# Side steps handed out by an account of the engines' time; context keys in column parts, value sums transposed

## The chip, the cores and the metric

The kernel runs on one core of a Trainium2 chip. A core has five engines with instruction streams of their own: TensorE (PE in the profile; its weight loads are shown apart as PEld), VectorE (DVE), ScalarE (ACT), GpSimd (POOL) and SyncE (SP), which here only issues transfers. Engines wait for each other by semaphores; each takes its instructions in order, so an instruction that waits holds everything behind it on that engine. The metric is the device time of one execution in microseconds, lower being better.

## The reference

One decoder layer over x of 16 batches x 256 positions x 512 columns, in float32:

```
x = x + mamba2(layernorm(x))                 # state space mixer, 32 heads of 64, state 64
x = x + attention(layernorm(x), context)     # 16 heads with sigmoid queries and keys
x = x + ffn(layernorm(x))                    # 512 -> 2048 -> 512, ternary weights, 8-bit activations

# mixer
xz = x @ W_in;  z, xBC, dt = split(xz)
xBC = silu(causal_conv4(xBC));  dt = softplus(dt + dt_bias);  A = -exp(A_log)
h_t = exp(A dt_t) h_(t-1) + dt_t x_t B_t;   y_t = h_t C_t + D x_t
y = norm_w * rms_normalised(y * silu(z));   out = y @ W_out

# attention
qh = sigmoid(q @ wq + bq);  kh = sigmoid(k @ wk + bk);  vh = k @ wv + bv
kv = einsum('bsh,bshd->bhd', kh, vh);  state = cumsum(kv, axis=1)       # over the heads
out = einsum('bsh,bhd->bshd', qh, state) @ wo + bo
```

## The kernel before

The 16 batches are worked in 8 pairs. The mixer's 2048 inner columns are cut into 16 units of 128, so its main loop has 128 slots (`for s in range(2, n_slots)`, L1927): slot s is unit s % 16 of pair s // 16. The last stage, the feed-forward layer (`ffn`, L1663), follows the 128 slots.

**A slot on TensorE**, in order: the projection of unit u0 to z (12 products of 512 columns, with the four transposes `trx` of the previous unit's x in the middle, L676 and L941); the projection to x (12 products); `scan_out` of the previous unit (`py`, L961 and L968); `out_product` of the one before (`po`, L1011, 12 products). **On VectorE**: `times_g` of the previous unit (L929, L933), `scan` of u0 (two scans, L912), three convolution taps on `xs` (L693), `plus_dx` (L976), `gated` (L981). ScalarE does the SiLUs, the convolution's first tap, the scaled copies `xdt` and `m`, the rounding `yh` and the squares; GpSimd does `yl` and the sum of squares.

**Side steps.** All other work of the layer lies between these: the norms of a later pair (`norm_pair`, L660), its time steps (`time_steps`, L698: with two long VectorE steps on tiles `sp_s`, L735 to L739, and `sp_q`, L742 to L745, and two exponentials on ScalarE that need another function table), its B and C states (`states`, L777: three taps on `bcT`, then `pg`, the products of B and C, L815), the end of a finished pair's batches (`batch_end`, L1049: norm, queries `q`, product `pa` with the attention's matrix z), the context keys and value sums (`context_pair`, L1201, and `context_group`, L1299), and the preparation of the feed-forward weights (`ffn_sums`, `ffn_quantised`). Each is a generator that yields before each step a wait, the points at which it may go on, an engine and a price in microseconds (helpers at L224 to L263).

**How they are placed.** The program is written out in full when it is built, and a slot has 8 points at which `advance(now)` (L1726) lets the generators issue steps. VectorE's steps may go at points 1, 2, 5 and 6, ScalarE's at 0, 5 and 6, GpSimd's at 2, 5 and 6, TensorE's at 3 (between the x projection and `scan_out`) and 7 (after the out product). `due` (L1714) holds a step back until its wait, a fixed distance of mostly 2 to 4 points after the step before, is over, and until its price fits what is left of its engine's budget (`room`: VectorE 2.3 us, ScalarE 2.5, TensorE 2.0, GpSimd 2.5); budgets are renewed at points 3 and 7. A step marked `leaves` (it empties a PSUM bank) is not held back by the budget. Transfers have a budget of their own.

**Banks.** Side products need a PSUM bank from `Banks` (L288): at point 7 one bank of their own, at most every half slot, in order of request; at point 3 they take, as "z", one of the two banks that the projections use in turn (`ps_p`). Then the next z projection uses the bank that the taps of the current x have just left. A pair's transposed input is held in two sets of tiles (`turned`), of which one is freed in slot 15 of each pair.

**Starting points.** `plan(s)` (L1763) starts the norms, time steps and states of pair k + 2 in slot 13 of pair k, the context pairs in slots 0 and 8 of the odd pairs, and a finished pair's batch ends in slot 2 of the next pair; `rank` orders the generators at each point.

**Context pair** (L1201 to L1296), for two batches: keys times weights in four column parts of the array (`pk`, L1225), moved to SBUF as `kp`; four products with `kp` as stationary and the 16 columns of `pick` streamed (L1246), which sum the four parts; a copy, tanh and scaling to `kh`; the key-weighted sums of the context in four column parts, one for each batch and half (`ptt`, L1264); a copy of 512 columns to `tt`; four products of `tt` with the selecting matrix `sel` (L1277), which transpose and add the halves, and the key sums (L1283); two copies into the group's tiles.

## Time and profile before

| what | value |
|---|---|
| median of three runs (lowest to highest) | 1882.19 us (1882.07 to 1885.43) |
| the profiled execution's own time | 1887.88 us |
| its span, first to last instruction | 1886.1 us |
| mean granted TensorE clock | 0.986 |
| PE, DVE, ACT, POOL busy | 95%, 87%, 66%, 36% of the span |
| pairs 1 to 6, length of each | 185.2, 190.2, 186.1, 185.2, 188.3, 183.4 us |
| the feed-forward stage | from about 1530 us to the end |

How to read it: busy is the time with an instruction of that engine in work, as the profiler has it. Matmuls overlap in a pipeline (a product of 512 columns is recorded with 0.38 us but starts every 0.217), so a busy PE may still lose time between starts. An idle time of an engine is put down to whatever released it last. Lengths of pairs are taken between the first `y<-xs,d_sb,py` (L976) of each.

### The profile page before, as it was taken

How to read it: one execution, taken by the hardware profiler on the slowest of the kernel's cores; microseconds unless marked ns; L12 is line 12 of the kernel's file. 1: busy time of each engine (PE TensorE's matmuls, PEld its weight loads, DVE VectorE, ACT ScalarE, POOL GpSimd, SP SyncE). 2: the span in 40 equal slices, each digit the busy share in tenths (PEclk: the TensorE clock that was granted, in tenths of full speed). 3: DMA queues.
4: the chain of work that ended last, by engine and by line, in shares of the span. 5: the costliest groups of instructions: out<-in, count | busy, mean ns of one | idle time of the engine just before them, and what ended most of it. 6: DMA issues, size and time to landing. Idle time of an engine off the chain costs nothing.

```text
span 1886.1 us, 30373 instructions
## 1 busy us (share of the span) xinstructions
PE 1786.5 (95%) x10464; PEld 1018.1 (54%) x10464; DVE 1638.2 (87%) x2711; ACT 1248.1 (66%) x2896; POOL 682.2 (36%) x691
## 2 busy tenths in 40 slices
PE   6789999998999998999999999998999989999998
PEld 4445555555556555555555555565656544444443
DVE  6989888777888889888988998989887888999997
ACT  5777666675666666666666666666666557777775
POOL 1233432344434354546454636463533222211000
PEclk8999999999999999999999999999999999999999
DMA  5764776788768777877597879787867734655454
GB/s 163 240 185 136 235 191 174 217 257 223 168 196 270 201 196 235 258 192 191 185 268 211 199 205 252 202 193 186 238 188 213 250 89 99 133 123 130 108 120 95
DMA packets 296933, 358.95 MB, mean 190 GB/s; under 512 B 163765, under 2 KB 197861, under 8 KB 296778
## 3 DMA queue, kind: packets, MB, share of 16 engines
q1 hardware_dynamic: 277962, 296.13, 60.0%
q0 software_dynamic: 18240, 60.84, 9.4%
q8 instruction: 83, 1.36, 0.3%
q14 instruction: 72, 0.59, 0.1%
q10 hardware_dynamic: 576, 0.04, 0.0%
HBM read 279.70 MB, written 39.58 MB: 169 GB/s over the span
## 4 chain that ended last, share of the span: by engine, by line
PE 57%; DVE 25%; DMA 7%; ACT 5%; issue 4%; POOL 2%; SPq 1%; ACTq 0%; POOLq 0%; DVEq 0%
PE pp L676 21%; PE po L1011 11%; PE po_f L1621 5%; PE pg L1579 4%; PE pu L1579 4%; DVE m L912 4%; DVE xs L693 4%; PE py L961 4%; DVE m L929 2%; PE trx L941 2%; DMA w<-w_d 2%; PE py L968 2%; DVE m L933 1%; DVE sp_q L742 1%; DVE y L976 1%
## 5 line engine op out<-in xcount | busy, mean ns | idle before, releaser
L676 PE MATMUL pp<-lnT_h_m,w 128*128 128x512 f16 (+1 forms) x2056 | 661.1, 383 | 23.3 <-DVE xs L693 20.8
L676 PEld LDWEIGHTS <-w 128*128 128x128 f16 x3084 | 296.5, 99 | 364.3 <-issue 35.8
L988 POOL TENSOR_TENSOR yl<-y,yh 128x512 fp32r<-128x512 f32 x128 | 178.9, 1398 | 717.5 <-ACT yh L987 659.3
L693 DVE SCALAR_TENSOR_TENSOR xs<-pp,convw_sb,xs 128x510 f32<-128x510 f32 (+2 forms) x384 | 286.1, 745 | 151.1 <-ACT xs L897 141.6
L676 PE MATMUL pp<-lnT_l_m,w 128*128 128x512 f16 (+1 forms) x1028 | 393.4, 383 | 0.0
L1011 PE MATMUL po<-wout,yh 128*128 128x512 f32 x1024 | 337.0, 410 | 4.6 <-DMA wout<-wout_d 4.6
L951 ACT ACTIVATE xdt<-trx,dt 128x64 f32<-128x64 f32 x1024 | 223.5, 328 | 167.4 <-PE trx L941 167.3
L912 DVE TENSOR_TENSOR_SCAN m<-dab,starts 128x512 f32<-128x512 f32 x254 | 302.2, 1230 | 0.5 <-DMA dab<-da_d 0.5
L1011 PEld LDWEIGHTS po<-wout,yh 128*128 128x128 f32 x1024 | 183.8, 189 | 61.3 <-issue 15.1
L1011 PE MATMUL po<-wout,yl 128*128 128x512 f32 x512 | 203.7, 398 | 3.0 <-POOL yl L988 3.0
L906 ACT ACTIVATE xs<-xs 128x512 f32<-128x512 f32 x128 | 80.9, 632 | 186.3 <-DVE xs L693 186.3
L961 PE MATMUL py<-m,xdt 128*64 128x256 f32 x1024 | 162.1, 395 | 11.1 <-DVE m L933 5.2
L1579 PEld LDWEIGHTS <-yT 128*128 128x128 bf16 x1024 | 100.0, 98 | 131.1 <-issue 14.7
L920 ACT ACTIVATE m<-edb,m 128x128 f32<-128x128 f32 x508 | 162.7, 395 | 12.1 <-DVE m L912 12.1
L999 POOL TENSOR_TENSOR ssq<-ssq,sq 128x512 f32<-128x512 f32 x120 | 158.6, 1321 | 27.9 <-ACT sq L998 27.0
L897 ACT ACTIVATE xs<-pp,convb_sb,convw_sb 128x512 f32<-128x512 f32 x128 | 100.3, 783 | 102.2 <-PE pp L676 102.1
L929 DVE TENSOR_TENSOR m<-m,g 128x1024 f32<-128x1024 f32 x128 | 161.9, 1265 | 0.1
L1579 PE MATMUL pg<-w_ffn,yT 128*128 128x512 bf16 x512 | 132.3, 381 | 4.7 <-ACT h L1583 4.7
L1579 PE MATMUL pu<-w_ffn,yT 128*128 128x512 bf16 x512 | 132.3, 381 | 4.6 <-DVE x L1037 4.6
L1621 PE MATMUL po_f<-w_ffn,hT 128*128 128x512 bf16 x512 | 125.4, 379 | 2.0 <-DMA hT<-hq 2.0
L1583 ACT ACTIVATE h<-pg,sg 128x512 f32<-128x512 f32 x128 | 86.6, 683 | 51.6 <-PE pg L1579 51.3
L1011 PEld LDWEIGHTS po<-wout,yl 128*128 128x128 f32 x512 | 96.7, 189 | 29.7 <-POOL yl L988 6.4
(278 smaller groups left out, 2791.9 us busy)
## 6 DMA issues: line engine op xcount, KB each, us to landing
dab<-da_d SPq DMA_DIRECT2D x127, 512.0 KB
wout<-wout_d SPq DMA_DIRECT2D x112, 512.0 KB
edb<-ed_d SPq DMA_DIRECT2D x127, 256.0 KB
w<-w_d SPq DMA_DIRECT2D x40, 512.0 KB
raw<-in_w_zx SPq DMA_DIRECT2D x16, 512.0 KB
wout_d<-wout SPq DMA_DIRECT2D x16, 512.0 KB
ctxT<-in_ctx_t POOLq DMA_DIRECT2D x16, 512.0 KB, 7.8
x<-in_x SPq DMA_DIRECT2D x16, 512.0 KB
```

The costliest lines, as they stand in the source:

```text
L676: nc.tensor.matmul(dst, w(wi, kc), yT[yi][:, :, kc, :], start=n == 0, stop=n == 3 * KD - 1)
L693: nc.vector.scalar_tensor_tensor(u[:, :, d:S], raw[:, :, 0 : S - d], w[:, j : j + 1], u[:, :, d:S], ALU.mult, ALU.add,)
L912: nc.vector.tensor_tensor_scan(u["m"][:, 4 * j : 4 * j + 4, :].rearrange("p k t -> p (k t)"), u["da"][j].rearrange("p h i t -> p (h i t)") ...
L920: nc.scalar.activation(u["m"][:, 8 + n, :], u["ed"][:, n // 2, n % 2, :], AF.Copy, scale=u["m"][:, 2 * n, P - 1 : P],)
L929: nc.vector.tensor_tensor(m, m, gi.unsqueeze(2).to_broadcast([P, 2, 2, NT * P]), ALU.mult)
L951: nc.scalar.activation(u["xdt"][:, j, i, h, :], u["tr"][:, j, i, h * HD : (h + 1) * HD], AF.Copy, scale=dt[:, i, j, 2 * c + h : 2 * c + h ...
L961: nc.tensor.matmul(py[h * HD : (h + 1) * HD, j, :].rearrange("p (i t) -> p i t", i=NT), xdt[:, j, 0, h, :], m[:, 2 * (2 * j + h) : 9 + 2 * ...
L988: nc.gpsimd.tensor_tensor(lo, u["y"], hi, ALU.subtract)
L999: nc.gpsimd.tensor_tensor(pair["ssq"], pair["ssq"], sq, ALU.add)
L1011: nc.tensor.matmul(pair["po"][n], u["yhl"][yi][:, j, i * P : (i + 1) * P], w[:, wi, :], start=c == 0 and p == 0, stop=c == NU - 1 and p == 2,)
L1579: nc.tensor.matmul(dst, yT[:, kc, :], w_ffn[w + kc][:, cols], start=kc == 0, stop=kc == KD - 1)
L1621: nc.tensor.matmul(u["po"], u["hT", k // (KF // 2)][:, k % (KF // 2), :], w_ffn[2 * KD + k // NF][:, (k % NF) * D : (k % NF + 1) * D], sta ...
```

## The change

**1. An account of the engines' time** (`Model`). While the program is written out, four clocks are kept for TensorE, ScalarE, VectorE and GpSimd. Each main operation of a slot adds its own duration, and starts no earlier than its inputs are reckoned to be ready; operations of VectorE that share SBUF access with GpSimd (`port`) and GpSimd's own don't overlap in it. From slot 18 to slot 127 (`modelled()`), a side step is handed out when `fits` says so: for VectorE when the next convolution taps still end by the end of the out products that cover them, for ScalarE and GpSimd when they stay within a bound behind TensorE, for TensorE when the inputs are reckoned ready and the taps stay in time (`Banks.take`). The slack grows with the slots that a step is overdue and near its task's `deadline`. The distances between steps become at most one point for steps of an engine, and the budgets are not asked any more, but for transfers; the points and the order of the banks stay. The prices in the steps themselves stay, too.

**2.** A pair's norms, time steps and states start in slot 12 instead of 13 (`AHEAD`).

**3.** `pg`, three products of 128 columns, becomes two: one of 256 and one of 128.

**4. Context pair**: `pick`, now 32 columns, becomes the stationary operand and `kp` is streamed, in four column parts; tanh reads PSUM; one transpose brings the keys back. The value sums are computed with columns instead of halves in the parts, accumulating over the halves, so that 256 columns are moved out instead of 512; two transposes take the place of the four products with `sel`, and four small copies that of two.

The diff, cut to its core (the other lines of the same kind: each main operation adds its duration with `model.op`, each `bank.take` names its product's duration, each `start` a deadline):

```diff
+        class Model:
+            def __init__(self):
+                self.t = dict.fromkeys(("pe", "act", "dve", "pool"), 0.0)
+                self.port, self.pool = [], []
+                self.proj, self.turn = [0.0, 0.0], 0
+                self.tp = 0.0
+            def op(self, engine, us, *after, port=False):
+                start_ = max([self.t[engine]] + [a + 0.1 for a in after])
+                if port:
+                    for a, b in self.pool[-6:]:
+                        if a <= start_ < b:
+                            start_ = b
+                            break
+                    self.port.append((start_, start_ + us))
+                elif engine == "pool":
+                    for a, b in self.port[-8:]:
+                        if a < start_ < b:
+                            start_ = b
+                            break
+                    self.pool.append((start_, start_ + us))
+                self.t[engine] = start_ + us
+                return start_ + us
+            def bank(self):
+                self.turn = 1 - self.turn
+                return 1 - self.turn
+            def convolved(self, dve, x_end):
+                return max(dve, max(x_end, self.t["act"]) + 0.9) + 2.3
+            def urgent(self, task):
+                return 0.5 * max(0, clock[0] / POINTS - task.deadline + 5)
+            def fits(self, task, moment, us):
+                t, e = self.t, task.engine
+                slack = 0.3 + 0.25 * max(0, clock[0] - task.due) / POINTS + self.urgent(task)
+                if e == "dve":
+                    if moment < 3:
+                        taps = self.convolved(t["dve"] + us, t["pe"] + X_US)
+                        end = t["pe"] + X_US + Y_US + OUT_US
+                    else:
+                        taps = self.convolved(
+                            t["dve"] + us + G_US + SCAN_US, t["pe"] + X_US + Z_US
+                        )
+                        end = t["pe"] + Z_US + X_US + Y_US + OUT_US
+                    return taps <= end + slack
+                if e == "act":
+                    return t["act"] + us <= t["pe"] + Z_US / 2 + 0.8 + slack
+                if e == "pool":
+                    return t["pool"] + us <= t["pe"] + (5.0 if moment > 3 else 9.0) + slack
+                return True
+        Z_US, X_US, Y_US, OUT_US, G_US, SCAN_US = 3.1, 2.6, 1.5, 2.85, 1.9, 2.45
+        model = Model()
+        current = [None]
+        def modelled():
+            return (NU + 2) * POINTS <= clock[0] < NP * NU * POINTS
...
-            def take(self, own=False, first=False):
+            def take(self, own=False, first=False, us=None, leaves_us=0.7):
                 me = [own]
+                task = current[0]
+                us = us or (task and task.pe_us) or 0.3
                 self.line.insert(0 if first else len(self.line), me)
+                asked = clock[0]
+                def fits():
+                    if not modelled():
+                        return True
+                    t, slack = model.t, 0.3 + 0.25 * (clock[0] - asked) / POINTS
+                    slack += model.urgent(task)
+                    if task.ready > t["pe"] + slack:
+                        return False
+                    if clock[0] % POINTS == 3:
+                        taps = model.convolved(t["dve"], t["pe"])
+                        return taps <= t["pe"] + us + Y_US + OUT_US + slack
+                    taps = model.convolved(
+                        t["dve"] + leaves_us + G_US + SCAN_US, t["pe"] + us + Z_US + X_US
+                    )
+                    return (
+                        self.free_at <= t["pe"] + slack
+                        and taps <= t["pe"] + us + Z_US + X_US + Y_US + OUT_US + slack
+                    )
                 while True:
                     moment = clock[0] % POINTS
                     if steady() and moment == 3:
                         others = [one for one in self.line if not one[0]]
-                        if self.free["z"] and others and others[0] is me:
+                        if self.free["z"] and others and others[0] is me and fits():
                             hold = "z"
                             break
                     elif self.free["own"] and self.line[0] is me and (
-                        not steady() or moment == 7 and clock[0] >= self.since
+                        not steady() or moment == 7 and clock[0] >= self.since and fits()
                     ):
                         hold = "own"
                         break
                     yield WAIT
...
-                for n, (s0, t0) in enumerate(((0, 0), (P, P), (0, P))):
+                for n, (s0, t0, t1) in enumerate(((0, 0, S), (P, P, S))):
                     nc.tensor.matmul(
-                        pg[:, n, :], bcT[0:NS, j, s0 : s0 + P], cT[:, j, t0 : t0 + P],
-                        start=True, stop=True,
+                        pg[:, 2 * n : 2 + n, :].rearrange("p n t -> p (n t)"),
+                        bcT[0:NS, j, s0 : s0 + P], cT[:, j, t0:t1], start=True, stop=True,
                     )
...
         def scan(u):
...
+                u["t_m"] = model.op("dve", 1.22, port=True)
...
+            hold = yield from bank.take(us=0.35)
+            pk = misc(hold, [P, P], f"pk2_{b}")
             for k in range(2):
                 for i in range(NT):
                     r = 64 * k + 32 * i
                     nc.tensor.matmul(
-                        pt[r : r + 32], kh[:, k, i, :], ct[k][:, i, :],
+                        pk[r : r + 32], pick, kp[:, k, i * P : (i + 1) * P],
                         start=True, stop=True, tile_position=(0, r),
                     )
-            yield leaves(dve(0.6))
-            tt = q1.tile([P, D], F32, tag="ttT", name=f"ttT_{b}")
+            yield leaves(act(0.3, 2))
+            khT = q1.tile([P, P], F32, tag="khT", name=f"khT_{b}")
+            nc.scalar.activation(khT, pk, AF.Tanh, scale=0.5)
+            bank.give(hold)
+            yield pe(0.2, 2)
+            hold = yield from bank.take(us=0.15)
+            pk = misc(hold, [P, 2, NT, 32], f"pk3_{b}")
+            nc.tensor.transpose(pk.rearrange("p k i h -> p (k i h)"), khT, ident)
+            yield leaves(dve(0.1))
+            nc.vector.tensor_scalar(
+                kh[:, :, :, 0:H], pk[:, :, :, 0:H], 0.5, 0.5, ALU.mult, ALU.add
+            )
+            bank.give(hold)
+            yield pe(0.5)
+            hold = yield from bank.take(us=1.0)
+            pt = misc(hold, [P, 2, P], f"ptt_{b}")
+            for i in range(NT):
+                for n in range(2):
+                    for k in range(2):
+                        r = 64 * n + 32 * k
+                        nc.tensor.matmul(
+                            pt[r : r + 32], kh[:, k, i, :],
+                            ct[k][:, i, :].rearrange("p (j n d) -> p n j d", j=2, n=2)[:, n],
+                            start=i == 0, stop=i == NT - 1, tile_position=(0, r),
+                        )
+            yield leaves(dve(0.4))
+            tt = q1.tile([P, 2, P], F32, tag="ttT", name=f"ttT_{b}")
             nc.vector.tensor_copy(tt, pt)
             bank.give(hold)
-            hold = yield from bank.take()
-            pt = misc(hold, [P, KD + 1, 4, 2, 4], f"ptk_{b}")
-            for kc in range(KD):
-                nc.tensor.matmul(
-                    pt[:, kc].rearrange("p q k h -> p (q k h)"), tt[:, kc * P : (kc + 1) * P],
-                    sel.rearrange("p q k h -> p (q k h)"), start=True, stop=True,
-                )
+            hold = yield from bank.take(us=0.6)
+            pt = misc(hold, [P, 2 * P + 2 * H], f"ptk_{b}")
+            for n in range(2):
+                nc.tensor.transpose(pt[:, n * P : (n + 1) * P], tt[:, n], ident)
+            sums = pt[0:1, 2 * P :].rearrange("p (k q h) -> p k q h", k=2, h=4)
             for k in range(2):
                 for i in range(NT):
                     nc.tensor.matmul(
-                        pt[0:1, KD, :, k, :], ones[:, 0:1],
+                        sums[:, k], ones[:, 0:1],
                         kh[:, k, i, 0:H].rearrange("p (q h) -> p q h", h=4),
                         start=i == 0, stop=i == NT - 1,
                     )
-            yield leaves(dve(0.2))
-            nc.vector.tensor_copy(
-                group["tt"][:, :, :, j : j + 2, :].rearrange("p c q k h -> p (c q) (k h)"),
-                pt[:, 0:KD].rearrange("p c q k h -> p (c q) (k h)"),
-            )
-            nc.vector.tensor_copy(group["ksum"][:, :, j : j + 2, :], pt[0:1, KD])
+            yield leaves(dve(0.3))
+            turned_ = pt[:, 0 : 2 * P].rearrange("p (c k q h) -> p c k q h", c=KD, k=2, h=4)
+            for k in range(2):
+                nc.vector.tensor_copy(
+                    group["tt"][:, :, :, j + k, :], turned_[:, :, k, 0:4]
+                )
+                nc.vector.tensor_copy(group["ksum"][:, :, j + k, :], sums[:, k])
             bank.give(hold)
             ctxs.give()
...
+            if task.engine and task.engine != "dma" and modelled():
+                if task.engine == "pe":
+                    if task.ready > model.t["pe"] + 0.3:
+                        return False
+                    task.pe_us = task.us
+                else:
+                    if not task.must and (
+                        task.ready > model.t[task.engine] + 0.2
+                        or not model.fits(task, now % POINTS, task.us)
+                    ):
+                        return False
+                    task.ready = model.op(task.engine, task.us, task.ready, port=task.port)
+                task.engine = None
+                return True
+            if modelled() and not task.engine and task.ready > model.t["pe"]:
+                return False
+            if task.engine == "pe":
+                task.pe_us = task.us
             if task.engine:
...
+                            task.port = task.engine == "dve" and not must
+                            if modelled() and task.engine and task.engine != "dma":
+                                wait = min(wait, 1)
+                            elif not task.engine and wait > 4:
+                                task.ready = 0.0
...
-            if (s == 1 or c == NU - 3) and k + ahead < NP:
+            if (s == 1 or c == NU - AHEAD) and k + ahead < NP:
                 pair = pairs[k + ahead] = {"k": k + ahead}
-                start(s, norm_pair(pair), rank=-4)
-                start(s, time_steps(pair), rank=-1 if k else -5)
-                start(s, states(pair), rank=-1)
+                first = (k + ahead) * NU
+                start(s, norm_pair(pair), rank=-4, deadline=first - 11)
+                start(s, time_steps(pair), rank=-1 if k else -5, deadline=first - 3)
+                start(s, states(pair), rank=-1, deadline=first)
...
-                    start(s, batch_end(batches[2 * ended["k"] + j]), rank=2)
+                    start(s, batch_end(batches[2 * ended["k"] + j]), rank=2, deadline=s + 12)
```

## The prediction

> **What bounds the kernel now.** First the clock: the core ran at a mean granted clock of 0.986, so there is no throttling to explain. Then the page's engine shares and slices, the stages in time, the waits of the stage that the change rewrites, and one bad slot beside a good one.
>
> ```profile
> PE 1786.5 (95%) x10464; PEld 1018.1 (54%) x10464; DVE 1638.2 (87%) x2711; ACT 1248.1 (66%) x2896; POOL 682.2 (36%) x691
> ```
>
> TensorE is the bound, with VectorE close behind. The change acts from slot 18 to slot 127 (about 280 to 1528 us). The stages there are the pairs 1 to 7, cut at the first `y<-xs,d_sb,py` of each; columns are stage, length, then busy us of PE, PEld, DVE, ACT and POOL:
>
> ```profile
> core 0: us, PE busy (x) PEld busy (x) DVE busy (x) ACT busy (x) POOL busy (x), PEclk, DMA share, GB/s
> 256.80:442.00 185.20, 178.04 (x1105) 105.61 (x1104) 144.00 (x204) 123.60 (x340) 67.51 (x77) 0.99 0.76 211
> 632.20:818.30 186.10, 177.97 (x1087) 106.31 (x1086) 164.75 (x231) 119.33 (x308) 91.01 (x90) 1.00 0.76 219
> 1191.80:1375.20 183.40, 176.80 (x1056) 105.37 (x1055) 165.40 (x235) 119.42 (x308) 89.60 (x80) 0.99 0.77 201
> 1375.20:1528.20 153.00, 151.05 (x888) 90.97 (x887) 132.01 (x189) 93.91 (x262) 44.88 (x37) 1.00 0.71 207
> ```
>
> A middle pair takes 183 to 190 us. Pair 7, with few side steps (15 slots up to 1528.2), runs at about 10.1 us a slot, or 161 for 16. The 25 us between them are side products on PE and waits. PE is uncovered for 6 to 8 us in each of the pairs 1 to 6, for 1.9 in pair 7. Who makes it wait between 280 and 1528 us (total, times, longest):
>
> ```profile
> PE pp L676 <- DVE xs L693: 20.2, 12, 3.4
> PE py L961 <- DVE m L933: 4.6, 5, 1.1
> PE po L1011 <- DMA wout<-wout_d: 4.6, 2, 4.3
> PE trx L941 <- ACT xs L906: 3.3, 4, 1.3
> PE pk L1246 <- DVE kp L1231: 2.4, 1, 2.4
> PE bc L676 <- ACT zs L891: 1.6, 1, 1.6
> ```
>
> So half of it is a projection that waits for VectorE's convolution taps. One such place in pair 6 (VectorE in order of time; then a quiet slot of pair 7):
>
> ```profile
> 1264.72 2.31 DVE L693 SCALAR_TENSOR_TENSOR bcT<-bc,convw_bc,bcT 128x510 f32<-128x510 f32 x3 [1.67 <-ACT bcT L791]
> ...
> 1268.68 3.37 DVE L912 TENSOR_TENSOR_SCAN m<-dab,starts 128x512 f32<-128x512 f32 x2
> 1271.97 1.25 DVE L735 TENSOR_SCALAR sp_s<-sp_v 128x128 f32<-128x128 f32 x1
> ...
> 1275.03 2.30 DVE L693 SCALAR_TENSOR_TENSOR xs<-pp,convw_sb,xs 128x510 f32<-128x510 f32 x3
> ...
> 1478.12 2.31 DVE L693 SCALAR_TENSOR_TENSOR xs<-pp,convw_sb,xs 128x510 f32<-128x510 f32 x3 [1.88 <-ACT xs L897]
> 1480.35 0.74 DVE L976 SCALAR_TENSOR_TENSOR y<-xs,d_sb,py 128x512 f32<-128x512 f32 x1
> ```
>
> Here 2.3 us of taps on `bcT` (must) and 3.1 us of `sp_s` (priced at 1.2) fell into one slot, and PE stood 3.44 us. PE then also runs slowly: the same 24 projections and 4 transposes took 5.41 us at clock 1.00 before this wait and 7.09 us at 0.76 after it:
>
> ```profile
> 1263.01:1268.42 5.41, 5.41 (x28) 2.73 (x28) 3.67 (x6) 5.35 (x14) 0.00 (x0) 1.00 1.17 169
> 1277.39:1284.48 7.09, 7.09 (x27) 3.46 (x28) 6.99 (x10) 5.47 (x14) 0.90 (x1) 0.76 0.43 157
> ```
>
> In the quiet slot VectorE idles 1.9 us even with a small side step. The taps end at 1480.4, the SiLU on them at 1481.15, the out products at about 1481.6, and the transposes that need the SiLU start at 1483.06: 1.9 us of slack.
>
> **The change part by part**, against the profiled execution (1887.88 us, span 1886.1; the three timed runs have a median of 1882.19, 5.7 lower; the same difference is taken off both).
>
> *The account: what it takes away.* The four waits it can see (20.2 + 4.6 + 3.3 + 2.4) are 30.5 us in 22 places. A wait is counted from the recorded end of the last matmul, 0.38 us after its start, where the next could start after 0.217: 0.17 hidden in each, 3.7 in all. The half speed after the long waits: 1.7 in the place shown, and by the starts of the projections about 0.8 after each of four more (two in pair 2, one each in 4 and 5): 5. Together 39. The two waits for `wout` stay, since transfers are not in the account.
>
> *What comes back.* The account uses the prices that stand in the steps. `time_steps` prices its two long VectorE steps at 1.2 and 1.7 us; the place above took 3.15 (1271.97 to 1275.12) and the second one 4.7 (1283.30 to 1288.03). The excess is 1.95 and 3.0 us. A step is accepted as long as the taps end by the end of the out products, so 1.2 to 1.5 of the 1.9 us slack may be used before it and 0.4 to 0.7 are left. Given at that limit the two cost PE 1.3 + 2.4 = 3.7 us a pair, given in an empty slot nothing; bounds 0 and 22 over six pairs, taken in the middle: +11.
>
> *Distances shortened.* Every wait of 2 to 4 points after an engine step becomes 1, so a side product on PE is issued as soon as its input is reckoned ready. Before, with 3 points between, side products waited for 2.4 + 1.6 + 0.7 (`pda` for ACT) + 0.5 (`q` for VectorE) = 5.2 us in the whole stretch. Behind a late one stand all of PE's products of the slot, then the taps and `plus_dx`. Bounds 0 and four times 5.2 = 21; I take +8, nearer the measured row because the points 3 and 7 lie 4 to 5 us apart and hide most errors.
>
> *Filling.* In pairs 3 to 6 VectorE is busy 165 us. If a pair shrinks from 185 to 177, its share is 93%, against 86% in pair 7 (132.01 of 153.00), where hardly a wait is left. Not every hole fits a step: bounds 0 and 10, taken +4.
>
> Together the account gives -39 + 11 + 8 + 4 = -16 us.
>
> *Context keys and value sums* (8 executions). Removed on PE: `pk2`'s 8 passes (729.83 to 730.75, 0.92 us) and `ptk`'s 8 passes with `sel` (771.32 to 772.23, 0.91). Added: four products of 128 columns in column parts. The nearest row is `ptt`, 512 columns in the same four parts in 1.00 us (760.34 to 761.34); a quarter is 0.25, at worst the 0.92 of what it replaces; I take 0.35. Also three f32 transposes at 0.11 (four `trx` in 0.43). `ptt` itself streams the same columns, 1.0. Net -1.83 + 0.35 + 0.33 = -1.15, times 8 = -9; bounds -10 and -5. VectorE: 0.21 + 0.32 + 0.67 + 0.28 + 0.17 go; 0.32, a 256-wide copy at 0.40 (the row `g<-pg,upper`), two of 64 at 0.21 and two `ksum` at 0.17 come: -0.2, nothing. ACT's tanh goes from 64 to 128 columns, 0.24 to 0.31: nothing, ACT is idle a third of the time. The extra bank turn and the ACT step between two PE steps are in the +8.
>
> The row for a column-part block's edges: from the last `ptt` product to the next main product it takes 0.2 us more than that one's spacing. [...]
>
> *`pg` in two products*: 6 passes took 742.74 to 743.60, 0.86; now 4 passes over the same columns: between 0.57 and 0.86, taken 0.70; 16 times, -2.
>
> *The rest.* AHEAD 4 starts the loads and norms of a pair a slot earlier. The transposed tiles are still freed only in slot 15, so nothing on the path moves. The step's 2.2 us on VectorE (priced 1.7), its POOL subtraction (2.15) and its SP load and transposes change place alone; SP waits there mostly for `dab` and `edb` buffers (272 and 269 us), which are two slots ahead. Cost 0; if that cover went, a late `lnT` would hold `time_steps` back and the taps would collide as now. POOL's own DMA issues (0.55 to 0.74 each) are not in the account; `yl` stands behind them, but 4 to 5 us before its product.
>
> The clock was 0.76 after the 3.44 us wait, but 1.00 (5.41 us again) after one of 2.67 us in pair 3. [...]
>
> Sum: -16 - 9 - 2 = -27. Profiled 1887.9 - 27 = 1861; median 1882.2 - 27 = 1855.
>
> **The rivals.**
>
> *Slower: the margin is spent everywhere.* Today a quiet slot has 1.9 us before the transposes. The account allows the taps to fall to the end of the out products in every slot that has side work (94 of them, 18 to 111). What it does not price (VectorE waiting for POOL: scans of 3.37 instead of 2.33, `sp` steps of 1.25 instead of 0.3) then reaches PE directly. A loss of w us in each takes the place of the +11: -39 - 9 - 2 + 8 + 4 + 94 w, which is nothing at w = 0.40 and decides from there on. At 0.5 us it is +9 (1891), at 0.6 +18 (1900), at 0.8 +37 (1919); I give it 1886 to 1919, around 1895. For it: VectorE at 89% in pairs 3 to 6. Against: 78% and 83% in pairs 1 and 2, and side work of VectorE averages under 2 us a slot where 2.5 are free.
>
> *A smaller gain: loads overtaken.* Transfers are not in the account. `ctx` lands a median of 7.7 us after its issue (at most 10.4), `wo` 7.3 (9.9). With one-point distances their products can follow a slot (10.1 us) later, POOL's issue itself may be late, and a wait for them holds all of PE. About 20 such products (6 `ctx`, 3 `wo`, some 12 `z`) at 0.5 to 1 us: +10 to +20, so 1865 to 1875. Against: the bank's line alone keeps steps two to four points apart.
>
> *A larger gain.* All waits but `wout` vanish: -39 - 5 - 9 - 2 = -55: 1827.
>
> *It does not do what it says.* Points and bank order stay as they are, so the steps may fall where they fell; then only the products count, and half of them hide in VectorE's slots: -5 to 0: 1877 to 1882.
>
> **How the numbers follow.** Forecast (1838 to 1868) 0.46; larger gain (1822 to 1838) 0.10; loads overtaken or little change of place (1868 to 1878) 0.14; within 0.2% (3.8 us, about what a measurement can tell) 0.07; slower 0.23, somewhat over a third of it (0.09) above 1893. The range 1832 to 1893 leaves out half the larger gain and that third, 0.14. The likeliest case's own range is 1838 to 1868. Faster 0.70, same 0.07, slower 0.23.
>
> **What would show it.** Right: pairs 3 to 6 at 179 to 183 us; the wait of the projections for `xs` under 8 us in the stretch; no stage with a clock of 0.76; in slots 4 to 8 of a pair `sp_s` no longer in the slot of the `bcT` taps; `pk` and `ptk` blocks of 0.3 and 0.6 us. Wrong: many waits of 0.5 to 1 us at `trx` for ACT `xs` (margin spent), waits at `ptt`, `zp` or `pa` for a DMA (loads overtaken), side steps left over beyond 1550 us, where VectorE is at 90% and above.

## The result: 1926 us, slower by 2.3%

The changed kernel takes 1926.49 us (median of six runs, 1924.13 to 1936.94), the kernel before, run beside it, 1884.15 (1882.07 to 1889.87): a ratio of 1.0229, 95% interval 1.0202 to 1.0256. The forecast was 1855, its range 1832 to 1893. The profiled execution took 1927.57 us against 1887.88, 39.7 more. Below, each run is given by its ratio to the kernel before, run beside it; "+17 us" means that ratio less one, times 1886.

The page's engine shares, then the stages (pairs 1, 3, 4, 6 and 7, cut as before; same columns) and the sum over pairs 1 to 7, all of the changed kernel:

```profile
PE 1789.4 (93%) x10456; PEld 1011.3 (53%) x10456; DVE 1660.9 (86%) x2717; ACT 1248.8 (65%) x2896; POOL 704.2 (37%) x690
```

```profile
256.30:453.00 196.70, 179.35 (x1098) 104.68 (x1097) 148.09 (x211) 124.35 (x342) 70.61 (x82) 0.96 0.72 210
...
651.50:845.60 194.10, 181.30 (x1147) 106.56 (x1146) 180.21 (x240) 125.84 (x316) 119.29 (x114) 0.98 0.80 234
845.60:1039.50 193.90, 179.81 (x1070) 106.54 (x1068) 178.73 (x252) 128.05 (x319) 115.49 (x104) 0.97 0.79 202
...
1228.10:1411.60 183.50, 175.84 (x1051) 104.45 (x1050) 161.09 (x224) 110.60 (x295) 55.06 (x45) 1.00 0.66 180
1411.60:1567.30 155.70, 150.71 (x885) 89.89 (x885) 132.08 (x187) 94.01 (x262) 47.76 (x37) 1.00 0.73 198
sum 1311.00, PE 1230.80 PEld 728.59 DVE 1120.39 ACT 833.21 POOL 579.97; mean PE 175.83 PEld 104.08 DVE 160.06 ACT 119.03 POOL 82.85
```

The seven pairs take 1311.0 us instead of 1271.4 (256.8 to 1528.2): the whole 39.6 us lie here. PE is busy for 1230.8 us, before for 1229.0, so the time is PE standing idle: 80 us instead of 42. Pairs 1 to 4 lose 8 to 12 us each; pair 6 is as before, pair 7 longer by 2.7. Who makes PE wait, between 275 and 1567 us of the changed kernel (total, times, longest):

```profile
PE pp L785 <- DMA w<-w_d: 13.7, 2, 11.0
PE trx L1060 <- ACT xs L1020: 12.1, 9, 2.8
PE pq L1151 <- POOL ssq L1125: 7.8, 2, 4.3
PE py L1083 <- DVE m L1050: 6.6, 5, 2.4
PE ptk L1409 <- ACT zs L1002: 4.6, 2, 2.8
PE pd L819 <- ACT zs L1002: 4.1, 1, 4.1
PE q L1206 <- DMA lnT_l_q<-lnl_q: 4.0, 1, 4.0
PE pp L785 <- DVE xs L802: 4.0, 6, 1.3
PE q L1206 <- ACT zs L1002: 3.2, 1, 3.2
PE kv L1456 <- ACT zs L1002: 3.0, 1, 3.0
```

With the smaller rows of the same view, grouped and set beside the view of before (us):

| what PE waits for | before | after |
|---|---|---|
| taps (`xs` of VectorE) | 20.2 | 4.0 |
| the rest of the scan chain (`trx`, `m`, `kp`) | 10.3 | 18.7 |
| a transfer (`w`, `wout`, `lnT`) | 6.1 | 20.5 |
| ScalarE's SiLU on z, by a side product (`zs`) | 2.3 | 18.2 |
| GpSimd's sum of squares (`pq`) | 0 | 7.8 |
| others | 1.9 | 8.4 |
| sum | 40.8 | 77.6 |

The account did what it was made for: the projections wait 4.0 us for taps, not 20.2. But all other waits together grew by 53 us. Two of them in the chain of waits. Late in pair 1 (start, length, what):

```profile
395.19 11.57 DMA z_d<-zh
...
406.82 13.63 DMA w<-w_d
...
420.49 2.74 PE pp L785 x6
```

SP's own queue shows why the load of `w` was issued so late, at 406.82:

```profile
394.50 3.43 SPq L1531 DMA_DIRECT2D z_d<-zh  x4
397.97 6.75 SPq L1531 DMA_DIRECT2D z_d<-zl  x4
...
406.82 0.83 SPq L521 DMA_DIRECT2D w<-w_d  x1
```

Eight stores of the attention's matrix z, issued in one point, take SP 10.2 us, and the load of `w` for the next projection stands behind them. By the chain, what let it go in the end was the landing of one of these stores, 11.57 us after its issue: SP's transfers wait here on eight semaphores in turn, mostly each for the transfer eight before it (the store issued at 395.19 and this load have the same one). In the kernel before, the load went 10 us ahead of the same stores:

```profile
395.76 0.42 SPq L412 DMA_DIRECT2D w<-w_d  x1
...
405.81 2.52 SPq L1400 DMA_DIRECT2D z_d<-zh  x4
408.43 4.52 SPq L1400 DMA_DIRECT2D z_d<-zl  x4
```

And in pair 4 of the changed kernel, the chain and then ScalarE's own row (in brackets its idle time and what ended it):

```profile
913.65 12.81 DMA wchunk<-in_w_up_t
...
928.10 1.53 ACT xdt L1072 x7
929.63 0.59 ACT zs L1002
...
930.26 0.77 PE q L1206 x24
```

```profile
926.48 1.52 ACT L1605 ACTIVATE wchunk<-wchunk,magic,wscale 128x512 f32<-128x512 f32 x2 [2.24 <-DMA wchunk<-in_w_up_t]
```

A chunk of the feed-forward weights lands 12.8 us after its issue. ScalarE has been given the step on it too early and waits 2.2 us, as it had waited 2.1 us for another chunk just before; behind these steps stand the main loop's `xdt` and the SiLU on z, and behind the SiLU stands PE, for 3.2 us, since its side product needs the bank that the SiLU empties. ScalarE's waits for these loads (same stretch) are 36 us in all, against 12 before; the three largest rows:

```profile
ACT wchunk L1570 <- DMA wchunk<-in_w_down_t: 12.1, 4, 5.8
ACT wchunk L1605 <- DMA wchunk<-in_w_gate_t: 10.6, 3, 4.9
ACT wchunk L1570 <- DMA wchunk<-in_w_up_t: 5.8, 4, 4.5
```

These steps are asked for six points after their load is issued (`landed(6)`), before as now. What is new is who lets them go: not a budget of ScalarE that other steps may have used up, but an account that gives them out as soon as ScalarE has time, by its reckoning; after a wait for a landing it sets `task.ready = 0.0`, that is, it takes the chunk to be there.

### The profile page after: what moved, and what is told of

Read it like the earlier page. It is cut to its first block, busy times and chain, and to the rows that moved or that the text cites. A ratio compares the mean times of both kernels' runs of the same rounds, so it can differ in the third digit from the quotient of the medians.

```text
span 1925.7 us, 30372 instructions
## 1 busy us (share of the span) xinstructions
PE 1789.4 (93%) x10456; PEld 1011.3 (53%) x10456; DVE 1660.9 (86%) x2717; ACT 1248.8 (65%) x2896; POOL 704.2 (37%) x690
## 4 chain that ended last, share of the span: by engine, by line
PE 50%; DVE 25%; DMA 7%; ACT 7%; issue 6%; POOL 4%; SPq 1%; ACTq 0%; POOLq 0%; DVEq 0%
PE pp L785 17%; PE po L1138 9%; PE po_f L1752 5%; PE pu L1710 5%; PE pg L1710 5%; DVE m L1027 5%; DVE xs L802 4%; PE py L1083 3%; DVE m L1046 2%; ACT xdt L1072 2%; PE trx L1060 2%; DVE y L1105 2%; PE py L1090 1%; DVE m L1050 1%; DMA w<-w_d 1%
## 5 line engine op out<-in xcount | busy, mean ns | idle before, releaser
L1113 POOL TENSOR_TENSOR yl<-y,yh 128x512 fp32r<-128x512 f32 x128 | 184.7, 1443 | 743.9 <-ACT yh L1112 653.7
L1027 DVE TENSOR_TENSOR_SCAN m<-dab,starts 128x512 f32<-128x512 f32 x254 | 324.3, 1317 | 0.0
L1036 ACT ACTIVATE m<-edb,m 128x128 f32<-128x128 f32 x508 | 164.3, 400 | 21.8 <-DVE m L1027 21.7
```

The source lines that it names most:

```text
L1027: nc.vector.tensor_tensor_scan(u["m"][:, 4 * j : 4 * j + 4, :].rearrange("p k t -> p (k t)"), u["da"][j].rearrange("p h i t -> p (h i t)") ...
L1036: nc.scalar.activation(u["m"][:, 8 + n, :], u["ed"][:, n // 2, n % 2, :], AF.Copy, scale=u["m"][:, 2 * n, P - 1 : P],)
L1113: nc.gpsimd.tensor_tensor(lo, u["y"], hi, ALU.subtract)
```

## The experiments

Four questions: which part costs (A), whether the unseen transfers do (B), what a mere change of the order of the side steps costs (C), and what is left when the account's blind spots are mended (D, E). "Moved" is how many of the 2650 to 2820 side instructions of pairs 1 to 7 lie in another slot than in the kernel before, counted from the two traces; where exactly a slot is cut shifts these counts by up to a tenth.

### A. The parts, each alone

`e1_products`: the changed kernel without the account and with the old starting slot.

```diff
 def modelled():
-    return (NU + 2) * POINTS <= clock[0] < NP * NU * POINTS
+    return False
-AHEAD = 4
+AHEAD = 3
```

> The column-part keys, transposed value sums and pg in two products, with the account never in force (budgets and distances as before, norms from slot 13). If the loss lies in the account, as the changed kernel's waits say, this is 4 to 11 us faster than before: 1873 to 1880, with the pk2 and ptk blocks on PE at 0.3 and 0.6 us. [...]

Measured 1923.42 us, 1.0178 (1.0147 to 1.0208): +34 us, where a gain of 4 to 11 had been expected if the loss lay in the account; 1715 steps moved.

`e7_account_only`: the changed kernel with the context pair, `sel` and `pg` of before.

```diff
-    pk = misc(hold, [P, P], f"pk2_{b}")
+    pk = misc(hold, [P, 2, NT, H], f"pk2_{b}")
...
-    pt = misc(hold, [P, 2, P], f"ptt_{b}")
+    pt = misc(hold, [P, D], f"ptt_{b}")
```

> The changed kernel's account and earlier start, with the context pair and pg of before. The products alone measured 36 us slower than before. Theory D (the longer chain of the context pair, one bank turn and one ScalarE step more, is what costs, and the account adds little): this is at 1880 to 1895. Theory A (steps handed out on weight chunks that have not landed): it is at 1905 to 1925, with ScalarE's waits on wchunk above 25 us. My forecast for the account alone was 16 us faster than before, 1870.

Measured 1924.2 us, 1.0205 (1.018 to 1.0231): +39; 1720 moved.

`e8_keys_only`: the kernel before, with the keys in column parts (one transpose and so one bank turn more).

```diff
-    pk = misc(hold, [P, 2, NT, H], f"pk2_{b}")
+    pk = misc(hold, [P, P], f"pk2_{b}")
...
+    nc.scalar.activation(khT, pk, AF.Tanh, scale=0.5)
+    bank.give(hold)
+    yield pe(0.2, 2)
+    hold = yield from bank.take()
+    nc.tensor.transpose(pk.rearrange("p k i h -> p (k i h)"), khT, ident)
```

> Before, with only the context keys in column parts (pk2, tanh from PSUM, the transpose pk3 with its own bank turn). Theory D: this part carries the loss of the products alone, +20 to +40 us, with a wait of PE for khT of some 10 us and the rest in side products that come a turn later. Theory E (any shift in the order of the side steps costs, since the chain of waits depends on where they meet): between +5 and +40, with waits in other places than in the products alone.

Measured 1929.05 us, 1.0225 (1.0183 to 1.0266): +42; 1765 moved. Its PE waits, first rows:

```profile
PE pp L676 <- DVE xs L693: 25.3, 10, 3.9
PE py L961 <- DVE m L933: 10.0, 5, 6.2
PE pk L1259 <- ACT khT L1254: 8.6, 2, 5.3
PE pd L710 <- DMA lnT_h_m<-lnh_m: 6.6, 1, 6.6
```

`e9_sums_only`: the kernel before, with the value sums turned.

```diff
-    pt = misc(hold, [P, D], f"ptt_{b}")
+    pt = misc(hold, [P, 2, P], f"ptt_{b}")
...
+    for n in range(2):
+        nc.tensor.transpose(pt[:, n * P : (n + 1) * P], tt[:, n], ident)
```

> Before, with only the value sums turned (columns in the parts, two transposes for the four products with sel, no bank turn more). Theory D: the products' saving alone, 0 to -6 us against before. Theory E: the different prices of two steps (0.4 for 0.6, 0.3 for 0.2) move some steps, and the time by +10 or more.

Measured 1888.35 us, 1.0003 (0.9986 to 1.002): +1; 77 moved.

The account and the keys each cost about as much as the whole change, so the parts don't add. The new product's own wait (`pk` for `khT`) is 8.6 us of the +42; the rest is spread over waits at other places. What the three dear runs share is that some 1700 side steps lie elsewhere. e8 alone doesn't separate this from a cost of the keys' longer chain of steps (one bank turn more).

The account alone (e7) does not lose at the places shown above: PE waits there 2.4 us for `zs` and 6.8 for transfers, hardly more than before, and 29.8 for the taps and the scan chain (before 30.5). The waits that grew in e7 are at many other places, 24.4 us instead of 1.9; the largest is 8.0 for GpSimd's `yl`. So the account loses about as much time in other ways when the order is another; what e7 loses by is not resolved here, though the mends of D bring it, too, down to +11 (e21).

### B. The transfers that the account doesn't see

`e2_landed14`: the changed kernel; the steps on weight chunks wait 14 points for their load (in both places).

```diff
     t = weight_chunk(k)
-    yield landed(6)
+    yield landed(14)
```

> The changed kernel, but the steps that load a chunk of feed-forward weights wait 14 points for it instead of 6. Theory A (ScalarE is handed steps on chunks that have not landed: 36 us of its waits on wchunk against 12 before, with xdt and the SiLU of z behind them): these waits fall below 8 us, PE's waits for zs and for trx fall by half, 1926 becomes 1890 to 1905. Theory B (side steps are packed too densely in pairs 3 and 4, so that VectorE and GpSimd slow each other: VectorE 179 to 180 us busy there against 165): it gains too, since chunks are spread over more slots, but with VectorE busy falling to 165 to 170. Theory C (the account hands out products at point 3 without asking whether the z bank is free): under 5 us gained, 1921 or more.

Measured 1907.1 us, 1.0093 (1.0062 to 1.0123): +18, just outside the 1890 to 1905 of theory A. ScalarE's waits for chunks are gone, and PE's waits for `zs` are 0.6 us instead of 18.2. Its waits for transfers stay, at 23.7.

`e3_no_landing`: the same order of steps, but the chunks are loaded to a place nobody reads.

```diff
-    nc.gpsimd.dma_start(t, src)
+    nc.gpsimd.dma_start(sink_d[k % 4], src)
...
-    t, t, AF.Abs, accum_out=...
+    t, starts.rearrange("p k t -> p (k t)"), AF.Abs, accum_out=...
-    nc.scalar.activation(t, t, AF.Identity, ...)
+    nc.scalar.activation(t, starts.rearrange("p k t -> p (k t)"), AF.Identity, ...)
```

> The changed kernel with the same order of steps, but the chunks of feed-forward weights are loaded into a scratch area in memory and ScalarE's steps on them read a constant tile, so that nothing waits for these loads; the feed-forward weights are therefore computed from constants. Theory A: ScalarE's waits on wchunk vanish and 15 to 30 us go with them, 1896 to 1911. Theory B: the density is the same, so VectorE stays at 178 to 180 us busy in pairs 3 and 4 and the time at 1915 to 1927.

Measured 1909.11 us, 1.0115 (1.0085 to 1.0146): +22. Here the order is that of the changed kernel (26 of 2570 steps lie in another slot), so the 21 us less by the ratios, 17 by the medians, are what waiting for the chunks and their loads cost; 1909 lies in the range of theory A and below that of theory B (density alone). PE's waits for `zs` are 2.6 us. The other half of the loss stays.

`e5_z_bank`: a side product at point 3 is also held back until the account reckons its bank empty.

```diff
     if clock[0] % POINTS == 3:
+        if model.proj[model.turn] > t["pe"] + slack:
+            return False
```

> The changed kernel, and a product at point 3 is also held back while the account reckons the z bank occupied. Theory C: PE's 18 us of waits for ACT zs before side products go, 1905 to 1912. Theory A: the account does not know that ScalarE is late (it stands on loads), so it sees the bank free and changes little: 1920 to 1930, with waits for zs still above 10 us.

Measured 1931.74 us, 1.0221 (1.0184 to 1.0258): +42, nothing gained. Waits for `zs` remain (7.2 us at `ptt`, 5.9 at `q`). That is what its expectation named for an account that takes the bank to be empty, because it doesn't know that ScalarE stands still for a load; what the account reckoned at these places is not on record.

### C. Another order, nothing else

All four are the kernel before, without any account, with one small edit of the bookkeeping. (e12 and e13 also let 0.1 us more work into a half slot; e11 and e14 change only when or in what sequence steps are asked.)

```diff
 e11_later_context
-    start(s, context_pair(2 * k + 2), rank=1)
+    start(s, context_pair(2 * k + 2), 1, 4, rank=1)
 e12_price (first ScalarE step on a chunk)
-    yield act(0.8, 0)
+    yield act(0.7, 0)
 e13_room
-    room = {"dve": 2.3, "act": 2.5, ...}
+    room = {"dve": 2.4, "act": 2.5, ...}
 e14_rank
-    start(s, batch_end(batches[2 * ended["k"] + j]), rank=2)
+    start(s, batch_end(batches[2 * ended["k"] + j]), rank=0)
```

> Before, with nothing changed but that in the odd pairs the first context pair may begin at point 4 of its slot instead of point 0. No product, price or distance differs. Theory D: within 0.5% of before (1875 to 1895). Theory E: a different order of side steps alone moves the time by 10 to 40 us.

> Before, with one number changed: the price of ScalarE's step in the sums of the feed-forward weights is 0.7 instead of 0.8 us. No product, transfer or distance differs, but about a quarter of VectorE's side steps come to lie in other slots, as many as with the new context keys. Theory E (before has an order in which few waits meet, and nearly any other order costs about 2%): +15 to +45 us. Theory D (the loss belongs to the longer chain of the context pair): within 0.5% of before, 1878 to 1897.

> Before, with VectorE's budget 2.4 instead of 2.3 us; about a fifth of VectorE's side steps come to lie in other slots. Theory E: +10 to +45 us. Theory D: within 0.5% of before, 1878 to 1897.

> Before, with the batch ends ahead of the other side steps (rank 0 for 2); about a quarter of VectorE's side steps come to lie in other slots. Theory E: +10 to +45 us. Theory D: within 0.5% of before, 1878 to 1897.

| run | median us | ratio (95%) | us | moved |
|---|---|---|---|---|
| e11_later_context | 1888.85 | 1.0014 (0.9999 to 1.003) | +3 | 146 |
| e13_room | 1898.05 | 1.0067 (1.0044 to 1.0089) | +13 | 977 |
| e12_price | 1902.98 | 1.0086 (1.0062 to 1.011) | +16 | 1525 |
| e14_rank | 1911.52 | 1.0138 (1.0111 to 1.0165) | +26 | 1683 |

These kernels do the same work as before, and no step of it is dearer. The three that moved many steps lie in the ranges of theory E and outside those of theory D; e11, which moved few, does not. With e9 above (77 moved, +1) they stand in one row: the more steps are redealt, the slower, up to 26 us. The order of before looks like a good draw among those tried. In e12 most of the loss is the wait for taps (20.2 us before):

```profile
PE pp L676 <- DVE xs L693: 30.1, 16, 3.4
```

### D. The blind spots mended

Three mends on the changed kernel: 14 points for the chunks (as in e2), the stores of z one for each point, and the two long VectorE steps of `time_steps` near their measured price.

```diff
     nc.sync.dma_start(z_d[g][k, c : 8 : 4], ...)
+    yield 1, range(POINTS), None, 0
...
-    yield dve(1.2)
+    yield dve(2.5)
...
-    yield dve(1.7)
+    yield dve(3.6)
```

`e15_mended` has all three, `e16_spread_only` and `e17_prices_only` one each. `e18_price_after` and `e19_price_mended` are the changed and the mended kernel with the edit of e12, which mends nothing.

> The changed kernel with three of its blind spots mended: 14 points for the weight chunks to land, the eight stores of z spread over eight points instead of issued together on SP's queue (with the 11 us wait for w behind them), and prices of 2.5 and 3.6 us instead of 1.2 and 1.7 for the two long VectorE steps of time_steps. Theory A (the account fails where it does not see): 1880 to 1895, with waits for w below 5 us, for xs and trx below 10 together. Theory E: the order is another again, so it lies anywhere between 1895 and 1930.

> The changed kernel; the only edit: the eight stores of a batch's attention matrix z are issued one for each point instead of all at one point. Theory (the account does not see the transfer queues): the wait of 11 us for the load of w behind these stores goes, and the eight main-loop waits for w of the changed kernel come down to under 5 us; 1926 becomes 1912 to 1918. Rival (only the mends together give a favourable order): within 4 us of 1926. Second rival (any other order moves the time by 10 us and more): below 1910 or above 1930 without the wait of 11 us accounting for it.

> The changed kernel; the only edit: the two long VectorE steps of the time steps are priced 2.5 and 3.6 us, near their measured 3.1 and 4.7, instead of 1.2 and 1.7. The prediction put the underpriced steps at +11 us; if that is right, 1926 becomes 1912 to 1918, and the waits of the projections and transposes for xs fall by about 8 us. Rival (the account's slack hides them): within 4 us of 1926. Second rival (any other order moves the time by 10 us and more): a difference over 15 us, or one with a plus sign, that these waits don't account for.

> The changed kernel with a change that repairs nothing: the price of ScalarE's first step on a weight chunk (the sum of absolute values) goes from 0.8 to 0.7 us. It only shuffles which step falls where. If the time of 1926 is what the account costs whatever the order, it stays within 8 us (1918 to 1934); if 1926 is one unlucky order among many, it can come out anywhere between 1890 and 1930, and the gains of 17 to 19 us seen when the chunks' loads are taken out would be no larger than such a shuffle.

> The changed kernel with its three blind spots mended (chunk loads given 14 points, z's stores one for each point, the two long VectorE steps at their price), which took 1888.6 us, and the same shuffle as in the run before (0.8 to 0.7 us for ScalarE's first step on a weight chunk). If the mended account is worth its time by itself, it stays at 1881 to 1897; if 1888.6 was a lucky order, it goes back to 1900 to 1926.

| run | median us | ratio (95%) | us | against the changed kernel (+43) |
|---|---|---|---|---|
| e15_mended | 1888.62 | 1.0013 (0.9999 to 1.0026) | +2 | -41 |
| e16_spread_only | 1928.46 | 1.0224 (1.0202 to 1.0247) | +42 | -1 |
| e17_prices_only | 1910.73 | 1.0134 (1.0104 to 1.0165) | +25 | -18 |
| e18_price_after | 1941.75 | 1.0297 (1.0276 to 1.0317) | +56 | +13 |
| e19_price_mended | 1895.39 | 1.0038 (1.0023 to 1.0053) | +7 | -36 |

The PE waits of e15 and its pairs 1, 3 and 4:

```profile
PE pp L785 <- DVE xs L802: 12.4, 8, 2.7
PE py L1083 <- DVE m L1050: 7.9, 7, 2.4
PE pq L1151 <- DVE y L1099: 5.4, 1, 5.4
PE trx L1060 <- ACT xs L1020: 5.2, 6, 1.6
```

```profile
258.30:437.50 179.20, 175.33 (x1091) 102.94 (x1091) 147.67 (x210) 118.39 (x324) 63.42 (x70) 1.00 0.73 210
...
623.70:806.00 182.30, 176.79 (x1109) 104.59 (x1108) 154.97 (x224) 119.54 (x323) 68.50 (x70) 1.00 0.79 226
806.00:998.70 192.70, 177.61 (x1109) 105.81 (x1107) 182.57 (x248) 126.09 (x315) 110.97 (x93) 0.99 0.78 202
```

Together the mends give back 41 us, 49 between the two kernels with the edit of e12 (+56 and +7), and 28 between e7 and its mended form e21 (+39 and +11, see E). That is more than any redealing cost, and the accounts with the mends (e15 +2, e19 +7, e21 +11, e20 +20) and those with none (e7 +39, e5 +42, the changed kernel +43, e18 +56) don't overlap: the three blind spots together are what made the account lose. Nor were the waits of the changed kernel an accident of one order: in e18 PE waits 18.0 us for `zs` and 21.7 for transfers, almost as there (18.2 and 20.5), and in e15 4.0 and 2.0. How the loss divides among them is not shown, but for the chunks (e3). The mended kernel redeals 2288 steps against before and is not slower. By the rows of C a redealing of that size costs some 26 us, so the mended account may earn about as much, and no more; that is argued from the rows, not shown. Pairs 1 and 3 run at 179 and 182 us, lengths such as the forecast had named for pairs 3 to 6. Pair 4, with 111 us of GpSimd, takes 7.5 us more than before and pair 7 (158.0 us) 5.0 more, so that the seven pairs come out only 2.3 us shorter. That the packed rounding of weights makes pair 4 long is not shown: with the edit of e12 (e19) it takes 183.8 us with 101 us of GpSimd. The expectation of e15 had also named waits for `xs` and `trx` below 10 us together; they are 17.6.

The single mends must be read with care, since e18 shows that an edit that mends nothing moves the changed kernel by 13 us. What can be read is the wait that each was made for. In e16 the 11 us wait for `w` is gone and the time is not: `pq` waits 11.5 us instead of 7.8 and ScalarE's SiLU holds `q_t` for 5.7. In e17, the PE waits by the same view:

```profile
PE pq L1151 <- POOL ssq L1125: 11.5, 3, 4.8
PE pp L785 <- DVE xs L802: 10.8, 10, 1.8
PE pp L785 <- DMA w<-w_d: 8.4, 1, 8.4
...
PE trx L1060 <- ACT xs L1020: 4.5, 4, 1.6
...
PE py L1083 <- DVE m L1050: 2.2, 2, 1.8
```

`trx` and `py` wait 6.7 us instead of 18.7, but the projections wait 10.8 us for taps instead of 4.0, so the three rows together fall only from 22.7 to 17.5, and in e15, with the same prices, they come to 25.5. What the underpriced steps cost is better read in the trace of the changed kernel itself: of these 22.7 us, 10.4 are waits with over 1 us of steps on `sp_s` or `sp_q` on VectorE in the 11 us before them; in e17 these are 5.8, in e15 2.7.

### E. What is left

`e20_pool_price`: the mended account with ten points for the chunks, and GpSimd's rounding at 2.4 us. `e21_mended_no_context`: the mended account with twelve points, and the context pair, `sel` and `pg` of before, as in e7.

```diff
 e20_pool_price
-    yield landed(14)
+    yield landed(10)
-    yield pool(1.3)
+    yield pool(2.4)
 e21_mended_no_context
-    yield landed(14)
+    yield landed(12)
```

> The mended account (z's stores one for each point, the two long VectorE steps at 2.5 and 3.6 us), with 10 points for the chunks' loads and one more mend: GpSimd's rounding of a weight chunk is priced 2.4 us instead of 1.3 (it takes 1.74 and issues a store of 0.55). In the version of 1888.6 us GpSimd is busy 111 us and VectorE 177 to 183 us in pairs 4 to 6, where VectorE waits for the shared port; with the higher price the rounding is spread out. If density in pairs 4 to 6 is what is left to lose, pair 4 (192.7 us) falls below 186 and the time to 1874 to 1884. Rival (the order alone decides what is left): 1885 to 1900, no relation to the pairs' VectorE time.

> The mended account (12 points for the chunks' loads, z's stores spread, the two prices) with the context pair, sel and pg as they were before. The prediction gave the products of the context pair and pg -11 us: if that holds under an account that knows the queues, this version takes 1895 to 1905. Rival (the shorter products are hidden or paid back by the extra bank turn): 1880 to 1892, not slower than the mended version of 1888.6. A shuffle alone moved the mended version by 7 us, so only a difference above that counts.

e20: 1907.89 us, 1.0105 (1.0076 to 1.0133), +20. Pair 4 takes 196.8 us with GpSimd still 105 us busy, so the higher price didn't thin it out; the time lies outside both of its ranges, and the question is not answered. e21: 1898.52 us, 1.0059 (1.0042 to 1.0077), +11, 9 us slower than e15. The shorter products of the context pair would be worth some 9 us by that, but two mended kernels with them differ by 5 to 7 among themselves and the number of points differs too: this stays open. No version beat the kernel before.

## Why the prediction was wrong, point by point

**The account, what it takes away: half right.** The taps fell from 20.2 to 4.0 us, as the term says. But 10.3 us of the 30.5 were the scans, `trx` and `kp`, and these rose to 18.7. The half speed was not saved either. By the starts of the projections, 26 of them before and 25 in the changed kernel followed the one ahead of them 0.3 us or more later without a wait, some 5 us above 0.217 in all each time: the term of 5 us had the right size, but other long waits took the place of those that went.

**Underpriced steps, +11: about right.** In the changed kernel 10.4 us of waits follow closely on these steps, most of them at `trx` and `py`. Mending the prices took 18 us off the time (e17), but an edit that mends nothing moved it by 13, so this isn't a measure of them.

**"Distances shortened", +8: the step that failed.** It was bounded by the side products' own waits of before (5.2 us), on PE alone. What lets a step go was taken to matter for that step alone, and for steps that wait for a transfer, on engines other than PE, nothing was put in. But an engine step given out early also holds the main loop's steps behind it, on ScalarE, GpSimd and SP, while it waits for a transfer. In the changed kernel 18.2 us of waits for `zs`, 20.5 for transfers and 7.8 at `pq` stand where 8.4 stood, +38; with the same order and nothing waiting for the chunks (e3) 17 to 21 us of the time are gone. The rival "loads overtaken" named the mechanism, but looked for it at PE's own products (`ctx`, `wo`, `z`) at 10 to 20 us; it came through ScalarE (weight chunks, 36 us of its waits) and through SP's queue. The chunk steps' own distance was not shortened: the budget that had held them back was gone. The start a slot earlier, put at 0, was never run alone, so that zero is open.

**What was missing altogether: the price of a new order.** The sum started from the waits of the kernel before and took off those that the account sees, as if the rest stayed. C shows that the rest depends on the draw: redealing 1000 to 1700 steps without any other change cost 13 to 26 us. That term, about +20 here, was missing from the sum. It may be a good part of why the keys, whose products got shorter, cost 42 us alone; at its largest (26), and with the new product's own wait (8.6), some 7 us of them stay without a name.

**The products, -11: nearly right as durations, not as time.** From its first product to the next one of the main loop, `pk` takes 0.36 us instead of 0.89 and 0.20 for the added transpose, `ptk` 0.59 instead of 1.19: -0.93, times 8, is -7.4 (forecast -9). `pg` takes 0.85 instead of 0.86: nothing (forecast -2), two products of 256 and 128 columns take as long as three of 128. The block in column parts took 0.36 with what follows it, about the 0.35 that had been taken. But e9 removes 0.6 us eight times from PE and measures +1 us (-3 to +4), so little or nothing of these 4.8 us reached the time.

**The signs named.** Pairs 3 to 6 at 179 to 183 us: 194.1, 193.9, 188.6, 183.5, wrong. `xs` under 8 us: 4.0, right. No stage at 0.76: after the 11 us wait a stage runs at 0.78, wrong. `sp_s` out of the slot of the `bcT` taps: so in five pairs of six (before in one), right. Of the wrong signs, `trx` for `xs` came in nine places, up to 2.8 us; waits for a DMA came, but at `pp`, `po` and `q`, not at `ptt`, `zp` or `pa`. No side work was left over beyond 1567 us that the kernel before does not also have there. One reading of the prediction was off without bearing on the sum: pair 7 takes 153.0 us for 15 slots, 10.2 a slot and 163 for 16, not 10.1 and 161.

**The slower rival** had the margin spent in each of 94 slots by 0.40 us or more. That is not what happened: `trx` waits in nine places. The side of the result was among the rivals, with 0.23, and its time lay beyond even that rival's 1886 to 1919; the reason is another. Of the others, "it does not do what it says" falls with 1867 moved steps, and the larger gain with the 77.6 us of waits.

## What to carry to other kernels

A planner that gives out work as early as it fits should know every resource that an instruction can wait for: queues and landings as well as engines, since one step given too early holds the main loop's steps behind it on its engine, as the step on a chunk did here on ScalarE for 2.2 us, with PE waiting 3.2 behind it. Budgets and distances that look like waste may be all that stands for those resources, so before taking them out ask what each has been covering. And before giving a cause to a change that redeals a static order, redeal the order with an edit that does nothing: here that alone moved the time by 13 to 26 us, as much as the single effects looked for.

## What the runs showed of the hardware

The length of a wait did not settle here whether PE fell to half speed, and the slow stretch could begin after the first products. After the 11.02 us wait the projections started 0.43 us apart from the first one on, and 0.22 apart only 5.0 us later:

```profile
420.49 0.61 PE L785 MATMUL pp<-lnT_h_m,w 128*128 128x512 f16 x1 [11.02 <-DMA w<-w_d]
420.89 0.63 PE L785 MATMUL pp<-lnT_l_m,w 128*128 128x512 f16 x1
...
425.71 0.59 PE L785 MATMUL pp<-lnT_h_m,w 128*128 128x512 f16 x2
426.14 0.38 PE L785 MATMUL pp<-lnT_l_m,w 128*128 128x512 f16 x1
```

After gaps of 3.07 and 3.93 us between starts (at 619 and 850 us) the first spacings of the projections were 0.22 us, then came some six slow ones, most of them 0.43; after gaps of 2.69 and 3.23 (522 and 1130 us) there was no slow stretch. So a gap of 3.07 us, 2.67 of them idle, was followed by a slow stretch, and one of 3.23, 2.85 of them idle, was not; nor was the wait of 2.67 us in pair 3 of the kernel before (717.19 us). What decides it is not shown.

Not expected either was how long SP takes over small stores: 10.2 us for the eight stores of z, of 64 KB each (7.1 in the kernel before), while a load of `w` of 512 KB that follows them takes it 0.83.

That some of VectorE's operations wait for GpSimd, which the account reckons with (`port`), shows in the times of one line of the kernel before: `gated` (`y<-y,zs`, L981) took 0.69 us in each of the 69 executions that met no GpSimd operation, and up to 1.99 us in the 59 that did. The taps (L693) took 0.72 to 0.75 us with and without one. What the two engines share is not shown by that.
